# A new order for the first four sequences of a transformer block with routed experts, and scaled heads written by GpSimd in the first

## The chip, the cores and the metric

The kernel runs on one core of a Trainium2 chip. Its five engines each work off their own queue in order: TensorE (PE for matmuls, PEld for the loading of weights into the array), VectorE (DVE), ScalarE (ACT), GpSimd (POOL) and SyncE (SP, which here only issues DMAs). They wait for one another by semaphores. The metric is the device time of one execution in microseconds, the median of several runs.

## The reference

There are 16 sequences of 256 tokens with 256 features. Each goes through attention with 16 heads of 64, q and k normalised head by head; then all 4096 tokens are routed to 8 experts, 512 tokens each.

```python
shift = silu(t) @ W_ada.T + b_ada
h = ln(x, ln1_g, ln1_b) + shift
qkv = (h @ Wqkv.T).reshape(b, n, 3, H, HD)
q = ln(qkv[:, :, 0], qn_g, qn_b); k = ln(qkv[:, :, 1], kn_g, kn_b); v = qkv[:, :, 2]
attn = softmax(q @ k.T / sqrt(HD))
x = x + (attn @ v) @ Wout.T
gate = softmax(x @ Wgate.T)
vals, idx = top_k(gate.T, tokens // E)
g = ln(x[idx], mlp_g, mlp_b)
y = gelu(g @ fc1s.T + b1s) @ fc2s.T + b2s
out = x.at[idx].add(y * vals)
```

## The kernel before

Everything is in fp32. The weights of q, k and v lie in SBUF as one tile, `wq`, of six groups of 512 columns: groups 0 and 1 are q, 2 and 3 are k, 4 and 5 are v. A sequence has two token tiles, t = 0 and 1. I write a group of a token tile as (g, t).

At the start the groups of q and k are centred in place: `center(g, c)` (L548) takes the mean of each head's 64 columns from the columns, one half of the 256 input features (c = 0 or 1) at a time, by a VectorE sum (L552) and a VectorE subtraction (L553). So the projected heads have mean zero, and the norm of a head needs only the sum of its squares.

The steps of a sequence are methods of small classes:

- `First` (L578): statistics of a token tile of x (L563 to L567), the power -1/2 on GpSimd (L82), the normalising on VectorE (L573), transposes (L597), and ScalarE's eviction to `hT` with gain and shift (L605).
- `Group` (L619), for (g, t): `matmul` (L631) projects into the PSUM tile `pm`; a matmul for each half of the features. For v, ScalarE copies `pm` out (L640). For q and k: `square` on ScalarE (L644), `stats` on VectorE (L648, L652), `power` on GpSimd (L82), `scale` (L664), `transposes` on TensorE (L673) and `evict` on ScalarE with gain and bias (L685).
- `Quad` (L693), for four heads: `scores` (L706), the row maxima on VectorE (L713), the exponentials with their sums on ScalarE (L722), the reciprocals (L729), the normalising on GpSimd (L733), transposes (L742), copies (L750 on VectorE, L752 on ScalarE), and the product with v (L760).
- `Tail` (L775): the output projection (L784), the residual, the store, the second norm and the gate.

A group of q or k has two forms of `scale`. Without `keep`, VectorE reads `pm` and writes the scaled heads to `qk`. With `keep`, ScalarE has first copied `pm` to `qk`, and GpSimd multiplies `qk` in place:

```python
def keep(self):
    self.qk = work.tile([P, GW], F32, tag="qk", bufs=3, name="qk")
    nc.scalar.copy(self.qk, self.pm)
```

`pm`, the transposed heads and the transposed tokens share one PSUM tag, "mm", of three buffers; the scores and the transposed probabilities share "sc", of four. There are three buffers of `qk`.

The order of the work is written out by hand, as places. Every step has a number; `at` (L1177) pairs the places of a class with its steps, and the list of all, sorted by number, is carried out in that order, each step adding its instructions to its engines' queues. A place says where in the queues a step stands; it isn't a time that anything waits for. `zip` in `at` pairs no step with a place that isn't there: a group with seven places has no `keep`, one with eight has.

`STEADY` (L146) holds the places of one sequence, shifted by `PERIOD` for each later one. `START` (L191) replaces them for the first sequences: wholly for 0 and 1, the norm and the groups for 2, the norm for 3. `END` does the same for the last ones. `SHIFT`, `CENTER`, `FILL` and `LOADS` (L302 to L305) place the shift, the centring, some transposes of the identity that only keep TensorE occupied, and the loads that ScalarE's queue issues (x of later sequences, half of `wq`, `wo`). Sequence 15 has groups of eight places, all others seven.

Of the kernel before, what the change touches and what calls it, by code (L numbers as in the profile page):

```python
# [43 lines left out]
def kernel(  # L44
# [81 lines left out]
    def make_others():  # L126
# [20 lines left out]
        first=((-88.131, -77.795, -66.865), (-86.413, -85.278, -65.341), (-64.291, -63.624)),  # L147
# [42 lines left out]
    )  # L190
    START = {  # L191
        0: dict(
            first=((-139.487, -139.084, -130.002), (-134.729, -123.135, -95.026), (-71.635, -61.204)),
            group={
                (0, 0): (-59.500, -57.180, -53.990, -41.905, -41.892, -31.199, -19.864),
                (0, 1): (-56.514, -46.937, -42.187, -36.541, -32.975, -14.723, -12.430),
                (1, 0): (-11.345, -10.160, -10.123, -9.363, -7.717, 16.862, 17.870),
                (1, 1): (-17.061, -12.458, -10.932, -9.433, -9.429, -7.544, -7.063),
                (2, 0): (-47.944, -39.268, -37.967, -29.426, -29.083, -19.329, -15.473),
                (2, 1): (-36.593, -35.280, -31.121, -27.896, -26.496, -20.716, -17.116),  # L200
                (3, 0): (-0.195, 1.354, 5.032, 6.866, 7.484, 18.359, 20.756),
                (3, 1): (-7.052, -4.047, -4.021, -2.780, 5.168, 9.583, 16.657),
                (4, 0): (-61.161, -56.511),
                (4, 1): (-24.033, -19.174),
                (5, 0): (8.030, 14.550),
                (5, 1): (-0.065, 4.397),
            },
            quad={
                (0, 0): (-9.254, 22.590, 42.649),
                (0, 0, 0): (-4.098, 3.192, 35.521, 40.175, 42.160),  # L210
                (0, 0, 1): (-7.788, -2.839, 22.830, 27.700, 30.119),
                (0, 1): (-10.825, 1.530, 42.650),
                (0, 1, 0): (-9.045, -8.059, 15.256, 16.378, 17.222),
                (0, 1, 1): (-6.921, -0.152, 15.562, 17.096, 23.635),
                (1, 0): (0.126, 14.031, 62.413),
                (1, 0, 0): (5.581, 9.438, 28.540, 45.916, 48.521),
                (1, 0, 1): (6.615, 11.701, 34.709, 42.123, 45.511),
                (1, 1): (6.647, 32.947, 62.414),
                (1, 1, 0): (12.684, 22.346, 38.667, 41.778, 42.977),
                (1, 1, 1): (16.709, 24.888, 35.995, 40.496, 41.536),  # L220
                (2, 0): (36.613, 44.084, 79.640),
                (2, 0, 0): (38.678, 40.096, 53.301, 75.810, 75.857),
                (2, 0, 1): (37.844, 41.179, 46.653, 73.800, 78.092),
                (2, 1): (31.788, 44.810, 79.641),
                (2, 1, 0): (35.309, 35.316, 47.104, 63.762, 75.398),
                (2, 1, 1): (35.999, 36.383, 45.887, 51.730, 53.463),
                (3, 0): (57.532, 66.273, 80.859),
                (3, 0, 0): (62.041, 62.092, 75.830, 76.948, 78.262),
                (3, 0, 1): (58.897, 62.045, 71.274, 78.272, 80.335),
                (3, 1): (42.288, 56.582, 80.861),  # L230
                (3, 1, 0): (53.169, 56.538, 74.699, 79.614, 79.641),
                (3, 1, 1): (55.287, 56.039, 56.589, 75.724, 78.348),
            },
            out=(52.169, 77.187, 79.720, 81.968),
            tail=((83.431, 83.938, 98.840, 128.374, 103.780, 103.911, 108.593, 110.466), (101.110, 104.350, 128.872, 145.215, 106.950, 107.929, 158.941, 161.116)),
        ),
        1: dict(
            first=((-46.775, -2.928, 1.521), (-17.063, -5.314, 0.982), (15.343, 17.672)),
            group={
                (0, 0): (18.719, 22.736, 28.212, 28.786, 33.289, 38.005, 45.577),  # L240
                (0, 1): (21.654, 25.091, 29.577, 30.657, 37.616, 45.616, 50.362),
                (1, 0): (56.965, 58.830, 59.835, 62.211, 62.315, 70.246, 74.608),
                (1, 1): (56.747, 57.357, 58.840, 58.862, 61.374, 62.457, 62.468),
                (2, 0): (40.127, 40.864, 42.252, 42.262, 45.473, 48.208, 52.717),
                (2, 1): (40.977, 41.918, 42.391, 45.462, 46.160, 49.170, 52.410),
                (3, 0): (74.826, 75.081, 75.503, 78.958, 80.988, 81.454, 84.690),
                (3, 1): (72.447, 74.612, 74.727, 79.840, 80.430, 81.825, 83.328),
                (4, 0): (36.938, 40.518),
                (4, 1): (52.802, 53.597),
                (5, 0): (63.613, 73.243),  # L250
                (5, 1): (30.152, 33.881),
            },
            quad={
                (0, 0): (80.434, 81.692, 98.968),
                (0, 0, 0): (80.662, 81.021, 85.076, 94.133, 94.171),
                (0, 0, 1): (80.458, 80.463, 87.029, 93.291, 94.064),
                (0, 1): (58.862, 78.602, 98.969),
                (0, 1, 0): (66.341, 68.024, 80.857, 85.468, 86.358),
                (0, 1, 1): (68.231, 73.899, 80.721, 81.679, 85.268),
                (1, 0): (80.676, 90.848, 105.478),  # L260
                (1, 0, 0): (81.477, 86.038, 92.163, 96.097, 96.147),
                (1, 0, 1): (82.096, 83.656, 93.097, 94.720, 94.811),
                (1, 1): (88.704, 93.176, 105.479),
                (1, 1, 0): (88.738, 92.999, 95.490, 103.218, 105.069),
                (1, 1, 1): (89.119, 89.714, 93.216, 99.811, 103.812),
                (2, 0): (87.127, 91.001, 112.620),
                (2, 0, 0): (87.343, 88.876, 92.124, 103.385, 105.927),
                (2, 0, 1): (87.397, 89.577, 94.021, 106.117, 107.673),
                (2, 1): (97.984, 99.909, 112.621),
                (2, 1, 0): (97.999, 98.450, 100.142, 107.055, 108.977),  # L270
                (2, 1, 1): (99.110, 99.138, 100.960, 105.621, 106.739),
                (3, 0): (104.738, 110.015, 121.526),
                (3, 0, 0): (105.837, 106.636, 110.756, 113.604, 116.432),
                (3, 0, 1): (106.309, 108.745, 110.059, 117.644, 117.997),
                (3, 1): (98.364, 104.978, 121.527),
                (3, 1, 0): (100.330, 101.404, 107.082, 108.878, 110.458),
                (3, 1, 1): (101.810, 102.324, 111.030, 115.380, 116.157),
            },
            out=(99.694, 108.037, 114.478, 121.947),
        ),  # L280
        2: dict(
            first=((14.779, 25.231, 54.912), (8.366, 37.062, 43.204), (56.764, 58.743)),
            group={
                (0, 0): (76.135, 78.537, 79.284, 80.073, 81.775, 92.853, 94.460),
                (0, 1): (86.065, 86.151, 86.371, 86.494, 90.513, 100.607, 102.738),
                (1, 0): (97.900, 98.023, 98.876, 99.334, 101.083, 108.588, 109.754),
                (1, 1): (99.552, 100.917, 100.935, 100.939, 103.765, 109.148, 114.215),
                (2, 0): (80.956, 82.580, 82.606, 83.027, 83.166, 86.029, 88.107),
                (2, 1): (92.816, 93.215, 94.312, 94.328, 98.305, 102.746, 104.145),
                (3, 0): (118.246, 120.897, 121.729, 121.739, 125.070, 134.647, 136.279),  # L290
                (3, 1): (104.183, 104.593, 105.142, 106.832, 107.066, 112.897, 117.208),
                (4, 0): (89.871, 89.886),
                (4, 1): (91.705, 92.213),
                (5, 0): (90.505, 91.515),
                (5, 1): (106.951, 108.771),
            },
        ),
        3: dict(
            first=((47.228, 83.201, 107.818), (73.608, 96.452, 102.635), (108.887, 108.932)),
        ),  # L300
    }
    SHIFT = (-103.533, (-96.272, -72.697), (-98.034, -88.980))  # L302
    CENTER = ((-64.072, -68.386), (-36.649, -27.859), (-57.938, -59.128), (-18.701, -14.089))
    FILL = (16, 4, 8, 12)
    LOADS = (-61.203, -19.863)  # L305


    END = {
        12: dict(
            tail=((747.192, 755.581, 778.455, 793.120, 768.716, 771.682, 797.160, 797.956), (784.519, 787.608, 791.406, 797.787, 789.463, 793.641, 821.185, 824.781)),  # L310
        ),
        13: dict(
            quad={
                (0, 0): (718.441, 730.722, 765.251),
                (0, 0, 0): (726.260, 726.660, 736.012, 745.374, 749.979),
# [160 lines left out]
    if True:  # L476
# [764 lines left out]
        first = Routing()  # L1241
# [151 lines left out]
```

## Time and profile before

| what | value |
|---|---|
| three runs | 1186.35, 1189.59, 1192.12 us; median 1189.59 |
| the profiled execution | 1187.28 us, its span 1185.6 us |
| granted TensorE clock, mean | 0.994 |
| instructions in the span | 19672 |
| POOL L82, power of 8 heads | 128 x 1656 ns |
| ACT L644, square, 128x512 | 128 x 600 ns |
| ACT L722, Exp, 128x256 | 512 x 474 ns |
| DVE L648, sum of squares | 128 x 683 ns |

The page of a profile gives the busy time of each engine, the span in 40 slices, the DMA queues, and the costliest groups of instructions with their mean time and the idle time before them. The trace behind it answers more: the same groups in a stretch of time, who waited for whom, and the instructions in order of time. PE's ends are modelled, since matmuls are pipelined; the distance from one start to the next is the firmer number. Times are from the start of the span.

In the first 60 us the profile has these:

| stretch, us | PE busy | DVE busy | ACT busy | POOL busy |
|---|---|---|---|---|
| 0 to 20 | 16.67 | 13.14 | 4.95 | 6.34 |
| 20 to 40 | 17.97 | 17.39 | 13.29 | 10.29 |
| 40 to 60 | 20.00 | 11.79 | 16.13 | 13.18 |

### The profile page before, as it was taken

To read this page: it belongs to the slowest core of one execution; us is meant where nothing else is said; L and a number is where in the kernel's file an instruction comes from. 1 tells how busy PE (TensorE), PEld (TensorE's weight loads), DVE (VectorE), ACT (ScalarE), POOL (GpSimd) and SP (SyncE) were. 2 spreads that over 40 slices of the span, in tenths; PEclk is the share of its full clock that TensorE was granted. 3 is DMA by queue.
4 is the path that set the end of the run, shared out by engine and by line. 5 is a ranking of instruction groups with operands and counts; after the bars stand their busy time and mean duration, and the time that the engine had idled before them with its cause. 6 is when DMAs were issued, how large, how long until landed. Compare 5 with 4: busy or idle time off the path is not lost. (4 is left out here: it accounts for less than half of the span.)

```text
span 1185.6 us, 19672 instructions
## 1 busy us (share of the span) xinstructions
PE 1157.4 (98%) x6823; PEld 817.5 (69%) x6823; DVE 759.0 (64%) x2303; ACT 630.4 (53%) x1721; POOL 585.4 (49%) x813
## 2 busy tenths in 40 slices
PE   8999999999999999999999999999988899999996
PEld 5566666666666666666666666677745788888885
DVE  7665676667566666666666666565588578755540
ACT  3856655566565656565655565656566333233331
POOL 3665464556556455555555545463672143333332
PEclk9999999999999999999999999999999999999998
DMA  6000000000000000000000000000110365666661
GB/s 197 1 1 6 5 19 19 10 19 10 19 23 6 23 10 19 10 23 6 23 10 27 10 10 9 19 14 19 61 39 1 113 190 183 187 187 187 183 187 21
DMA packets 46740, 62.41 MB, mean 53 GB/s; under 512 B 3889, under 2 KB 39985, under 8 KB 46641
## 3 DMA queue, kind: packets, MB, share of 16 engines
q1 hardware_dynamic: 36864, 49.03, 12.4%
q0 software_dynamic: 6144, 8.39, 3.9%
q10 hardware_dynamic: 3632, 3.74, 1.0%
q8 instruction: 54, 0.88, 0.3%
q14 instruction: 46, 0.37, 0.1%
HBM read 48.56 MB, written 12.58 MB: 52 GB/s over the span
## 5 line engine op out<-in xcount | busy, mean ns | idle before, releaser
L631 PE MATMUL pm<-wq,hT 128*128 128x512 f32 x768 | 361.8, 600 | 2.2 <-ACT qT L685 0.9
L733 POOL TENSOR_SCALAR pr<-pr,sums 128x256 f32<-128x256 f32 x512 | 236.9, 480 | 208.3 <-DVE sums L729 160.9
L82 POOL TENSOR_TENSOR ss<-ss,neghalf 128x8 f32<-128x8 f32 x128 | 211.8, 1656 | 184.7 <-DVE ss L652 180.0
L722 ACT ACTIVATE pr<-sc,nmax 128x256 f32<-128x256 f32 x512 | 236.2, 474 | 115.9 <-DVE nmax L713 108.3
L631 PEld LDWEIGHTS pm<-wq,hT 128*128 128x128 f32 x768 | 133.6, 190 | 123.4 <-issue 109.9
L713 DVE TENSOR_REDUCE nmax<-sc 128x2 f32<-128x512 f32 x256 | 166.7, 684 | 38.2 <-PE sc L706 38.1
L648 DVE TENSOR_REDUCE ss<-sq 128x8 f32<-128x512 f32 x128 | 87.4, 683 | 109.9 <-ACT sq L644 109.4
L742 PEld LDWEIGHTS pp<-ident,pr 128*128 128x128 f32 x1024 | 119.1, 142 | 48.2 <-POOL pr L733 21.0
L742 PE MATMUL pp<-ident,pr 128*128 128x128 f32 x1024 | 139.2, 274 | 0.1
L644 ACT ACTIVATE sq<-pm 128x512 f32<-128x512 f32 x128 | 76.7, 600 | 113.5 <-PE pm L631 110.1
L706 PE MATMUL sc<-kT,qT 64*128 64x256 f32 x1024 | 129.3, 390 | 0.0
L760 PE MATMUL po<-prT,v 128*64 128x256 f32 x1024 | 126.1, 389 | 0.0
L706 PEld LDWEIGHTS sc<-kT,qT 64*128 64x128 f32 x1024 | 93.3, 186 | 41.9 <-issue 31.1
L784 PE MATMUL pw<-wo,oT 128*128 128x256 f32 x512 | 117.8, 383 | 0.0
L1135 PE MATMUL ph<-xT,w 128*128 128x256 f32 x512 | 117.5, 382 | 0.0
L1151 PE MATMUL py<-w,hid 128*128 128x256 f32 x512 | 116.5, 380 | 0.0
L1168 POOL DMA_INDIRECT out<-y,idx x32 | 51.4, 1605 | 124.8 <-DVE y L1162 57.7
L784 PEld LDWEIGHTS pw<-wo,oT 128*128 128x128 f32 x512 | 96.7, 192 | 18.7 <-issue 6.5
L722 ACT ACTIVATION_READ_ACCUMULATOR pr<-sc,nmax 128x1 f32 x512 | 105.0, 205 | 0.0
L1142 ACT ACTIVATE hid<-ph,vec 128x256 f32<-128x256 f32 x128 | 60.2, 473 | 83.3 <-PE ph L1135 75.8
L1135 PEld LDWEIGHTS ph<-xT,w 128*128 128x128 f32 x512 | 95.4, 190 | 12.9
L1151 PEld LDWEIGHTS py<-w,hid 128*128 128x128 f32 x512 | 95.5, 190 | 12.7
(136 smaller groups left out, 1294.1 us busy)
## 6 DMA issues: line engine op xcount, KB each, us to landing
w<-in_fc2T SPq DMA_DIRECT2D x16, 1024.0 KB
w<-in_fc1T SPq DMA_DIRECT2D x16, 1024.0 KB
out<-tok SPq DMA_DIRECT2D x32, 128.0 KB
xn_dram<-tn SPq DMA_DIRECT2D x32, 128.0 KB
xs<-in_x SPq DMA_DIRECT2D x12, 256.0 KB
b<-in_b2s SPq DMA_DIRECT2D x16, 128.0 KB
wq<-in_wqkvT SPq DMA_DIRECT2D x3, 512.0 KB
wq<-in_wqkvT ACTq DMA_DIRECT2D x3, 512.0 KB
```

What stands on the lines that cost most here:

```text
L82: nc.gpsimd.tensor_tensor(dst, src, neghalf[:, : src.shape[1]], ALU.pow)
L631: nc.tensor.matmul(self.pm, hTs[self.b][:, c, bass.ts(self.t, P)], wq[:, c, bass.ts(self.g, GW)], start=(c == 0), stop=(c == DC - 1),)
L648: nc.vector.tensor_reduce(self.ss[:, 0, :], self.sq.rearrange("p (h d) -> p h d", d=HD), AX.X, ALU.add,)
L706: nc.tensor.matmul(self.sc[i, j][:, t, :], qTs[self.b][rows, hp, bass.ts(t, P)], kTs[self.b][rows, hp, :], start=True, stop=True,)
L713: nc.vector.tensor_reduce(self.nmax[i, j], self.sc[i, j], AX.X, ALU.max, negate=True)
L722: nc.scalar.activation(self.pr[i, j][:, t, :], self.sc[i, j][:, t, :], AF.Exp, bias=self.nmax[i, j][:, t : t + 1], scale=1.0, accum_out=se ...
L733: nc.gpsimd.tensor_scalar(self.pr[i, j][:, t, :], self.pr[i, j][:, t, :], self.sums[i][:, 1, j, t : t + 1], 1.0, ALU.mult, ALU.mult,)
L742: nc.tensor.transpose(self.pp[i, j][:, c, bass.ts(t, P)], self.pr[i, j][:, t, bass.ts(c, P)], ident,)
L760: nc.tensor.matmul(self.po[j * HD : (j + 1) * HD, i, :], vs[self.b][:, c, bass.ts(4 * self.d + 2 * i + j, HD)], self.prT[i, j][:, c, :], s ...
L784: nc.tensor.matmul(self.pw, oTs[self.b][:, hp, bass.ts(self.t, P)], wo[:, hp, :], start=(hp == 0), stop=(hp == HP - 1),)
L1135: nc.tensor.matmul(self.ph[f], self.w1[:, c, bass.ts(f, P)], self.xT[:, c, :], start=(c == 0), stop=(c == DC - 1),)
L1151: nc.tensor.matmul(self.py[i], self.hid[:, f, bass.ts(i, P)], self.w2[:, f, :], start=(f == 0), stop=(f == FC - 1),)
```

## The change

Only places change. The eight groups of q and k of sequence 0 get an eighth place, so `keep` runs for them and GpSimd scales them; and all places of the sequences 0 to 3 that `START` holds are new, as are those of the shift, the centring and the two sets of loads. The number of sequences, all sizes, buffers and steps are as before, and so are `STEADY` and `END`. The core of it:

```diff
         0: dict(
-            first=((-139.487, -139.084, -130.002), (-134.729, -123.135, -95.026), (-71.635, -61.204)),
+            first=((-133.593, -101.058, -97.256), (-158.376, -131.500, -104.051), (-81.952, -81.887)),
             group={
-                (0, 0): (-59.500, -57.180, -53.990, -41.905, -41.892, -31.199, -19.864),
-                (0, 1): (-56.514, -46.937, -42.187, -36.541, -32.975, -14.723, -12.430),
-                (1, 0): (-11.345, -10.160, -10.123, -9.363, -7.717, 16.862, 17.870),
-                (1, 1): (-17.061, -12.458, -10.932, -9.433, -9.429, -7.544, -7.063),
-                (2, 0): (-47.944, -39.268, -37.967, -29.426, -29.083, -19.329, -15.473),
-                (2, 1): (-36.593, -35.280, -31.121, -27.896, -26.496, -20.716, -17.116),
-                (3, 0): (-0.195, 1.354, 5.032, 6.866, 7.484, 18.359, 20.756),
-                (3, 1): (-7.052, -4.047, -4.021, -2.780, 5.168, 9.583, 16.657),
-                (4, 0): (-61.161, -56.511),
-                (4, 1): (-24.033, -19.174),
-                (5, 0): (8.030, 14.550),
-                (5, 1): (-0.065, 4.397),
+                (0, 0): (-80.466, -69.038, -57.316, -39.709, -38.352, -36.469, -35.382, -52.242),
+                (0, 1): (-60.059, -54.606, -54.600, -39.627, -32.905, -30.429, -30.229, -51.780),
+                (1, 0): (-30.395, -29.479, -6.942, 7.553, 11.559, 18.176, 30.532, -20.763),
+                (1, 1): (-33.879, -30.714, -22.761, -17.147, 0.473, 1.479, 6.362, -30.403),
+                (2, 0): (-51.648, -51.234, -47.356, -33.810, -32.220, -27.888, -16.240, -49.845),
+                (2, 1): (-39.169, -35.673, -32.084, -31.658, -31.069, -18.625, -11.081, -36.449),
+                (3, 0): (-15.423, -2.636, 4.458, 12.729, 16.826, 29.832, 31.195, 2.002),
+                (3, 1): (-20.569, -12.443, -7.775, 1.095, 1.104, 10.131, 14.846, -2.034),
+                (4, 0): (-81.874, -62.410),
+                (4, 1): (-47.993, -40.422),
+                (5, 0): (2.941, 10.417),
+                (5, 1): (-35.340, -32.229),
             },
             quad={
-                (0, 0): (-9.254, 22.590, 42.649),
+                (0, 0): (-10.378, 16.013, 65.445),
...
-                (0, 1): (-10.825, 1.530, 42.650),
+                (0, 1): (-1.606, 22.773, 65.446),
...
-    SHIFT = (-103.533, (-96.272, -72.697), (-98.034, -88.980))
-    CENTER = ((-64.072, -68.386), (-36.649, -27.859), (-57.938, -59.128), (-18.701, -14.089))
+    SHIFT = (-103.258, (-99.231, -92.324), (-94.650, -91.422))
+    CENTER = ((-91.311, -88.593), (-42.094, -51.590), (-84.871, -62.797), (-31.921, -44.332))
     FILL = (16, 4, 8, 12)
-    LOADS = (-61.203, -19.863)
+    LOADS = (-81.886, -35.381)
```

In the queues this means, for the first projections on TensorE:

```
before: (4,0) fill (0,0) (0,1) (2,0) (2,1) T(0,0) (4,1) T(2,1) T(2,0) (1,1) T(0,1) (1,0) scores ...
after:  (4,0) fill (0,0) (0,1) (2,0) (4,1) (2,1) T(0,0) (5,1) (1,1) T(0,1) (1,0) T(2,0) (3,1) T(2,1) (3,0) scores ...
```

T(g,t) stands for the transposes of the scaled heads.

## The prediction

> **What bounds the kernel now.** I read the engines' busy times first, then cut the span into stretches, then asked what TensorE waited for in the first 45 us.
>
> ```profile
> PE 1157.4 (98%) x6823; PEld 817.5 (69%) x6823; DVE 759.0 (64%) x2303; ACT 630.4 (53%) x1721; POOL 585.4 (49%) x813
> ```
>
> ```profile
> 0.00:12.00 12.00, 9.52 (x57) 8.04 (x58) 5.70 (x16) 2.53 (x4) 1.86 (x9) 1.00 0.82 262
> 12.00:32.00 20.00, 17.12 (x65) 8.55 (x65) 17.64 (x37) 8.84 (x14) 9.44 (x6) 1.00 0.42 135
> 32.00:45.00 13.00, 13.00 (x61) 7.61 (x60) 10.65 (x26) 11.73 (x37) 7.94 (x12) 1.00 0.00 1
> 45.00:850.00 805.00, 805.00 (x4655) 534.19 (x4654) 516.45 (x1170) 483.28 (x1381) 445.24 (x661) 1.00 0.04 14
> ```
>
> The columns are the stretch, its length, busy time of PE, PEld, DVE, ACT and POOL, granted clock, DMA. From 32 to 850 us TensorE is never idle, so there a new order can only lose. The stretch after 850 (336 us, 312.78 busy) is the end, which stays and moves along. What can be won lies before 32 us: 2.88 idle in 12:32 and 2.48 in 0:12.
>
> TensorE's waits in 0:45, as line, releaser, total, times, longest:
>
> ```profile
> PE pq L673 <- DVE qk L664: 1.3, 2, 1.0
> PE pm L631 <- ACT qT L685: 0.9, 1, 0.9
> PE pm L631 <- DVE wq L553: 0.7, 1, 0.7
> PE pm L631 <- DVE qk L664: 0.7, 1, 0.7
> ```
>
> A group's PSUM tile is read twice: ACT squares it, then, after DVE's sum and POOL's power, DVE scales it. The three "mm" tiles are held through that chain, so TensorE stands. One rule says otherwise of what bounds the kernel: the Trainium skill, Perfetto Trace Analysis, section Identifying the Most-Contended Engine, says that matmul busy time misjudges TensorE and weight-load busy time judges its room. By the rule 69% leaves 31% of room, some 360 us, and a better order could win much anywhere. But the weight loads of one projection start at 12.29, 12.71, 13.14, 13.57: one pass per 0.43 us, each with a load of 0.19 and 0.24 of "issue". That stream is full at 44% load. I take the row: no room after 32 us.
>
> **Costs used**, all from the timeline: a projection is four passes, 1.72 us, readable 2.02 after its start (11.75 to 13.77). Four transposes occupy 0.43 (42.05, 42.49, 42.93), readable after 0.66 (20.79 to 21.45). Eight score matmuls take 1.93 (37.10 to 39.03). ACT starts 512-wide work every 0.50 (13.77, 14.27), a head's eviction every 0.68. Centring half a weight group is two DVE instructions, 1.33. A power is 1.64. The new pair exists already, in the last sequence:
>
> ```profile
> L664 DVE TENSOR_TENSOR qk<-pm,ss x120: 658/681/693, 17.1 to 817.7; 128x512 f32<-128x512 f32 x120
> L664 POOL TENSOR_TENSOR qk<-qk,ss x8: 1042/1042/1228, 835.3 to 877.4; 128x512 f32<-128x512 f32 x8
> L626 ACT COPY qk<-pm x8: 580/584/620, 833.6 to 872.5; 128x512 f32<-128x512 f32 x8
> ```
>
> So DVE loses 8 x 0.68 = 5.4 us, ACT gains 8 x 0.58 = 4.7, POOL gains 8 x 1.04 = 8.3. POOL's sequence-0 line goes from 8 x 1.64 = 13.1 to 21.4. A PSUM tile is now free after two ACT instructions.
>
> **The new beginning, step by step.** Up to 9.16 nothing moves: same loads, shift, first transposes, first projection (4,0), and the 12 fills end at 11.06.
>
> *Centring.* Before, half 1 of group 0 was centred before half 0, and the projection begins with half 0, so it waited to 11.75. Now half 0 comes first (done 10.37), half 1 at 11.70, needed 0.86 after the start. (0,0) starts at 11.08: 0.67 won.
>
> *Projections.* (0,0) 11.08, (0,1) 12.80, (2,0) 14.52 (its weights centred at 14.35), (4,1) 16.24 (ACT has copied (0,0) away at 15.90), (2,1) 17.96 to 19.68. None waits.
>
> *First heads.* POOL: power of (0,0) 15.24 to 16.88, of (0,1) to 18.60, scale of (0,0) to 19.62. Its transposes run 19.69 to 20.12. Before they ran at 20.79 with one projection fewer done: TensorE is 1.1 + 1.72 = 2.8 us ahead.
>
> *The added waits.* There are three "qk" tiles, so ACT's copy of (2,1) waits for the transposes of (0,0) (20.35), with the square of (2,1), the eviction of (0,0) and the loads behind it; the square then gives DVE its sum at 21.45, while DVE is centring anyway.
>
> *A new stop.* (5,1) runs 20.15 to 21.87. Then (1,1) needs group 1 centred. DVE, from 16.96: half 1 of group 1, a sum, statistics of sequence 1, half 1 of group 3, half 0 of group 1: done 22.75. TensorE waits 0.9.
>
> *The port.* Here a rule speaks against the change. The Trainium skill, SBUF — State Buffer, section Who interferes with whom: a DVE instruction with two SBUF inputs and a GpSimd instruction that reads SBUF exclude each other for a whole instruction. Centring's second half (L553) has two. Against POOL's powers the trace shows nothing (L553 is 0.691 to 0.693 in all eight). Against POOL's scale there is one near row, a DVE product of two SBUF tiles:
>
> ```profile
> 854.69 2.23 POOL L664 TENSOR_TENSOR qk<-qk,ss 128x512 f32<-128x512 f32 x2
> 854.78 1.36 DVE L852 TENSOR_TENSOR gate_of<-gates,smax 128x224 f32<-128x224 f32 x1
> ```
>
> It ends 0.4 after the first of the two scales: it seems to have stood until then, and the scales lost 0.15 (2.23 against 2.08). So row and rule agree in kind; the size depends on who meets whom. The last centring (22.06) falls into the scale of (0,1), 21.26 to 22.28: by the row 0.22 late; without the rule 0; if it stood through the next scale too, 1.25. I take 0.2: TensorE resumes at 23.0.
>
> *To the scores.* (1,1), transposes of (0,1) (scaled 22.3), (1,0), transposes of (2,0) (23.3), (3,1), transposes of (2,1) (26.3), (3,0): all scaled 2.1 us or more before TensorE arrives, ACT's releases too. Four projections and three transposes are 8.2: scores start at 31.2. Before they started at 29.0 with 8 projections done; now 11 are, and as many transposes: 3 x 1.72 - 2.2 = 3.0 ahead. Before then loses 0.4 more at 31.4 (waiting for the scaled (1,1)): 3.4.
>
> *After the scores.* POOL's scales of (1,1), (3,1), (1,0) end near 31, 33.5, 36.2, each 2.3 to 3.5 before use. ACT becomes the late one. Its queue, in order: square and copy of (3,0) and (3,1), the Exp table load (1.28, at 29.74 before), two Exps, the copy of (3,0), two Exps, the eviction of (1,1), V, sequence 1's hT. On the copy of (3,0) hang sequence 1's first transposes; on the eviction, those of (3,1); on hT, the first projection of sequence 1. From the square of (3,0) at 31.5 I get: copy of (3,0) done 35.35, the second Exps 36.25, hT's first half 38.0, against TensorE's 35.28, 36.05, 37.5. Stops: 0.1, 0.2, 0.5. By 45 us: 3.4 - 0.8 = 2.6 ahead.
>
> *45 to 50.* The second eight scores need PSUM tiles that two more Exp pairs and a copy release at 46.9 and 47.4: 0.5. POOL waits for the first statistics of sequence 1 with three normalisations queued behind; their transposes come 3 us later. Sum: **2.1 us**.
>
> *Moved loads.* The x, wo loads on ACT's queue still follow the first head's eviction (21.45 before, 21.4 now). DVE asks for sequence 2's statistics earlier, at 24.8; x0 took 3.1 us from its issue at 0.79 to use, so x2 is there at 24.5. If not, the sums of (1,1) wait; they have 2 us. SP keeps its order but for two stores exchanged.
>
> DVE's 5.4 and ACT's 4.7 count nothing by themselves: neither sets the end. Of sequences 1 to 3 the order is new too; I found no number there, TensorE has 100% before, so the bounds are 0 and a loss. I take 0, as POOL (445 of 805 us) and ACT (483) have room in that stretch.
>
> **Sum.** The profiled execution took 1187.28 (span 1185.6); less 2.1 is 1185.2. The runs' median is 1189.59, 2.3 above it, within their spread of 1186.35 to 1192.12. So the forecast is 1187.5. About 0.5%, 5.9 us, is what a measurement can tell from no change, and this is 0.2%. The most that could come is 0.67 plus what TensorE loses between 11.75 and 45. By 43.47 it has done 12 projections, 8 head transposes, 16 scores and three more fours: 29.3; less the first two pieces (2.15) that is 27.15 in 31.72: 4.57. So 5.2 us, below 0.5%.
>
> **Rivals.**
> *Given back (0.27).* The order up to sequence 4 has stops that the old one hadn't: ACT's queue slips by a few more places like the one at hT. For it: ACT has 11.73 of 13 us in 32:45 and gets 3 of the copies there or just before. Against: later it has 40% free. A loss equal to the win gives 1189.6.
> *POOL becomes the line (0.12, the slower one).* Every scale blocks or is blocked by DVE's two-input work, and power plus scale are strictly in order. At 2 x 1.04 each, eight cost 8.3 more; 2.1 are slack; 6.2 stops against 2.6 won: 3.6 slower, 1193.2. It decides from 0.6 per scale on (8 x 0.6 = 2.1 + 2.6). With 0.69 before and after each, 11 - 2.1 - 2.6 = 6.3: 1195.9. For it: the 1.36 row. Against: only four centrings remain then, and the scales in the last sequence are 1.04 in the median.
> *The stops of this sum are larger (0.06).* The port 1.25 instead of 0.2, hT and the second scores 1.5 each instead of 0.5: 3.05 more, 1190.5.
> The forecast has 0.55.
>
> **Numbers.** The likeliest case alone runs from 1184.4 (all 5.2) to 1188.8. For 8 in 10 I take 1184.0 to 1192.5, which takes in given back, most of the POOL case and the runs' own spread. Faster by over 0.5% would need more than there is: 0.03, for a shifted median. Slower by over 0.5%: 0.09, the bad end of the POOL case and a stop in sequences 1 to 3 that I don't see.
>
> **What would show it.** TensorE's first long projection run starts near 11.1; first head transposes near 19.7; a wait on L553 of about 1 near 22; scores near 31.2; 12:32 busy near 18.9; no wait on L664 by POOL longer than 0.3. POOL's scales at 1.04 to 1.2 refute the slower rival; scales near 2 and TensorE waiting for them make me wrong, and so does idle TensorE between 45 and 220.

## The result, and the profile after

The changed kernel's median is 1184.52 us (5 runs, 1184.28 to 1187.2), that of before beside it 1190.09 (5 runs, 1186.35 to 1192.12); the ratio is 0.9959, with a 95% interval of 0.9943 to 0.9975. In a second comparison, with 9 runs against 31, it is 0.9972 (0.9960 to 0.9985). The change makes the kernel about 0.3 to 0.4% faster, 3.4 to 5.6 us in the medians. Forecast were 2.1 us. The profiled execution, though, took 1187.2 us with a span of 1185.5: it shows nothing of the gain against the 1187.28 and 1185.6 of before. That is the riddle of this case.

First the busy line of the page of the changed kernel, then its stretches (length, busy PE, PEld, DVE, ACT, POOL, granted clock, DMA):

```profile
PE 1160.5 (98%) x6823; PEld 820.6 (69%) x6823; DVE 755.6 (64%) x2295; ACT 634.3 (54%) x1729; POOL 595.7 (50%) x821
```

```profile
0.00:12.00 12.00, 10.54 (x44) 9.27 (x45) 6.22 (x17) 2.53 (x4) 1.87 (x9) 1.00 0.70 228
12.00:32.00 20.00, 19.38 (x67) 9.86 (x66) 14.90 (x34) 10.69 (x20) 14.17 (x12) 1.00 0.47 156
32.00:45.00 13.00, 13.00 (x64) 7.49 (x64) 7.65 (x19) 12.08 (x36) 11.66 (x13) 1.00 0.00 1
45.00:850.00 805.00, 805.00 (x4668) 535.12 (x4665) 518.08 (x1171) 484.80 (x1385) 447.22 (x661) 1.00 0.04 14
```

In 12:32 TensorE is now idle for 0.62 us instead of 2.88, and from 32 to 850 it never is, as before. Of its waits before 850 us, beside that for the first fill, one is left:

```profile
PE pm L631 <- ACT qT L685: 0.6, 1, 0.6
```

So the waits went as meant. What ate the gain stands ahead of 12 us. The timeline of TensorE in this execution:

```profile
5.14 1.86 PE L512 MATMUL pa<-sT,wa 128*128 128x16 f32 x8
6.84 1.09 PE L499 MATMUL fill<-ident 128*128 128x128 f32 x4
7.72 1.06 PE L597 MATMUL ph<-ident,xn 128*128 128x128 f32 x4
8.58 1.91 PE L499 MATMUL fill<-ident 128*128 128x128 f32 x8
```

Eight fills take 1.91 us here; in the profile of before they took 1.04, from 6.94 on. TensorE ran at half its speed until after 10 us here, and only up to about 5 us there. I call an execution warm early or warm late by this. The first long run of projections thus starts at 13.64, not at 11.1. The same kernel, profiled a second time:

```profile
5.14 1.03 PE L512 MATMUL pa<-sT,wa 128*128 128x16 f32 x8
6.03 0.63 PE L499 MATMUL fill<-ident 128*128 128x128 f32 x4
6.62 0.66 PE L597 MATMUL ph<-ident,xn 128*128 128x128 f32 x4
7.11 1.04 PE L499 MATMUL fill<-ident 128*128 128x128 f32 x8
...
11.06 2.31 PE L631 MATMUL pm<-wq,hT 128*128 128x512 f32 x5
```

To compare executions apart from this I use an anchor: the transposes of one later sequence's normed tokens (L597), which stand in the steady order of every kernel here; ahead of them each trace has the same 2202 matmul records, fills aside. The timeline near 400 us of before, of the changed kernel, and of its second profile:

```profile
406.30 0.60 PE L597 MATMUL ph<-ident,xn 128*128 128x128 f32 x4
```

```profile
406.06 0.60 PE L597 MATMUL ph<-ident,xn 128*128 128x128 f32 x4
```

```profile
403.92 0.60 PE L597 MATMUL ph<-ident,xn 128*128 128x128 f32 x4
```

With TensorE fast early in both, the changed kernel is 406.30 - 403.92 = 2.4 us ahead (3.0 ahead of before's second profile, whose first weights came later, see below). With TensorE fast late it is still 0.2 ahead of an execution of before that was fast early.

### The profile page after: what moved, and what is told of

Same layout as the page of the kernel before. It is cut to its first block, busy times and chain, and to the rows that moved or that the text cites. A ratio compares the mean times of both kernels' runs of the same rounds, so it can differ in the third digit from the quotient of the medians.

```text
span 1185.5 us, 19697 instructions
## 1 busy us (share of the span) xinstructions
PE 1160.5 (98%) x6823; PEld 820.6 (69%) x6823; DVE 755.6 (64%) x2295; ACT 634.3 (54%) x1729; POOL 595.7 (50%) x821
## 3 DMA queue, kind: packets, MB, share of 16 engines
q1 hardware_dynamic: 36864, 49.03, 12.5%
```

## The experiments

The table has each kernel's profiled execution (start of the first long run of projections, anchor, anchor less start) and all its runs. Before ran 84 times beside them: 1186.28 to 1192.35, mean 1189.5. Two theories on the variation between executions are named in what was expected: W puts it down to the moment near the start at which TensorE becomes fast, D to falls of the clock that short waits of TensorE bring. What they call equal warm-up is the comparison of executions that are both warm early or both warm late.

| kernel | start | anchor | difference | median of runs | ratio to before (95%) |
|---|---|---|---|---|---|
| before, first profile | 11.75 | 406.30 | 394.55 | 1190.09 | |
| before again | 12.37 | 406.91 | 394.54 | 1189.84 | 1.000 (0.9988 to 1.0012) |
| changed, first profile | 13.64 | 406.06 | 392.42 | 1184.52 | 0.9959 (0.9943 to 0.9975) |
| changed again | 11.06 | 403.92 | 392.86 | 1186.67 | 0.9972 (0.9960 to 0.9985) |
| centring only | 11.04 | 407.23 | 396.19 | 1189.76 | 0.9999 (0.9985 to 1.0012) |
| order without copies | 13.03 | 426.88 | 413.85 | 1206.13 | 1.0129 (1.0111 to 1.0146) |
| copies without order | 11.90 | 412.91 | 401.01 | 1194.01 | 1.0043 (1.0027 to 1.0059) |
| scales doubled | 10.96 | 408.71 | 397.75 | 1190.01 | 1.0004 (0.9994 to 1.0014) |
| group 1 centred early | 13.20 | 404.77 | 391.57 | 1184.98 | 0.9958 (0.9942 to 0.9973) |
| fewer fills | 10.34 | 403.16 | 392.82 | 1185.32 | 0.9972 (0.9960 to 0.9984) |
| before, gaps filled | 12.15 | 406.70 | 394.55 | 1187.40 | 0.9982 (0.9969 to 0.9995) |
| both mends | 11.04 | 403.62 | 392.58 | 1184.56 | 0.9964 (0.9950 to 0.9978) |
| three mends | 12.59 | 404.13 | 391.54 | 1184.56 | 0.9957 (0.9942 to 0.9973) |
| no first fills | 14.11 | 406.53 | 392.42 | 1187.41 | 0.9984 (0.9971 to 0.9997) |

### Before again, and changed again

No edit.

> The kernel before, unchanged. The changed kernel was 5.6 us faster in the medians, but its profiled execution took 1187.2 and starts its projections at 13.64 us, 2.6 later than I worked out: TensorE still ran each filling transpose in 0.22 us up to about 10 us, where the profile of before had 0.12 from 5 us on. Theory W (warm-up): the moment at which TensorE gets fast differs from execution to execution of one kernel and shifts all after it; then the times of this kernel spread over 4 us or more, with low ones near 1187 and high ones near 1190 to 1192, and an execution with late fast transposes is long. Theory O (order): the order alone is worth 5 us at equal warm-up and 1187.2 was a stray; then this kernel's times lie within 2 us of 1190. Both expect a ratio of 1.000.

> The changed kernel, unchanged. Theory W: where TensorE is fast from 5 us on, the first long run of projections starts at 11.1 and the span is near 1182.8; where it is fast only from 10 us on, 13.6 and 1185.5; at equal warm-up it is 2.1 to 2.9 us ahead of before. Theory O: 4 to 5.6 us ahead of before whatever the warm-up. Ratio 0.9945 to 0.998 in both.

Before's 14 runs spread over 5.3 us, from 1186.64 to 1191.96: that is a spread as theory W expects, but W is not shown to be its cause. The profiled execution, 1189.6, is 2.3 us longer than the first profile of before, and TensorE was warm early in both. What differs at the start is a wait for centring, which was 0.69 in the first:

```profile
12.37 5.42 PE L631 MATMUL pm<-wq,hT 128*128 128x512 f32 x12 [1.30 <-DVE wq L553]
```

VectorE's first centring sum, which waits for the load of `wq`, began at 9.58 instead of 8.96: 0.6 us come from there, and 1.7 from behind the anchor. None of the five profiles with before's beginning (the two here, centring only, copies without order, gaps filled) is warm late, so what late warmth costs before was not seen. The changed kernel's second profile has TensorE fast at 5 us and its long run at 11.06, as theory W has it, and is 2.4 ahead at the anchor, within 2.1 to 2.9. Its span missed: 1185.1 instead of 1182.8. What follows the anchor took 1185.1 - 403.92 = 781.2 there and 779.3 to 779.4 in the first profiles of both kernels; the order there is the same. So a further 2 us of variation lie in the end. Theory O, 4 us or more whatever the warm-up, is refuted by the anchor.

### Centring only

```diff
-    CENTER = ((-64.072, -68.386), (-36.649, -27.859), ...
+    CENTER = ((-68.386, -64.072), (-36.649, -27.859), ...
```

> The kernel before with one thing changed: of group 0, half 0 is centred before half 1. Theory W and the working of the prediction: 0.67 us where TensorE is fast early, nothing where it is fast late, since the fills then end after both halves are centred; ratio 0.9994 to 1.000, and the profile has no wait of TensorE on L553. If the centring is what set the beginning, 2 us or more.

The wait on L553 is gone and the first long run starts at 11.04, 0.7 earlier; the time is the same. The profile shows a second thing: the gaps that remain cost the clock. TensorE's timeline and the stretches of this kernel:

```profile
17.30 1.98 PE L631 MATMUL pm<-wq,hT 128*128 128x512 f32 x4 [0.94 <-DVE qk L664]
20.11 0.63 PE L673 MATMUL pq<-ident,qk 128*128 128x128 f32 x4 [0.82 <-DVE qk L664]
21.60 2.94 PE L631 MATMUL pm<-wq,hT 128*128 128x512 f32 x4 [0.87 <-ACT qT L685]
```

```profile
18.00:21.00 3.00, 1.92 (x7) 0.64 (x6) 2.93 (x7) 0.82 (x2) 1.83 (x3) 1.00 0.00 0
21.00:24.00 3.00, 2.40 (x4) 1.05 (x5) 2.93 (x6) 0.55 (x1) 1.56 (x1) 0.75 0.66 180
24.00:27.00 3.00, 3.00 (x12) 2.19 (x11) 2.64 (x6) 2.11 (x3) 0.00 (x0) 0.68 1.05 363
```

After three waits within 6 us the granted clock fell to 0.75 and 0.68 in two stretches of 3 us, and the projection at 21.60 took 2.94 instead of 1.98. The difference of the anchor is 1.6 us more than in the two profiles of before, which had waits of the same kind (0.66, 0.97 and 0.87 in both) and no fall of the clock. So such gaps sometimes cost a clock dip and sometimes don't.

### Order without copies

```diff
-                (0, 0): (-80.466, -69.038, -57.316, -39.709, -38.352, -36.469, -35.382, -52.242),
+                (0, 0): (-80.466, -69.038, -57.316, -39.709, -38.352, -36.469, -35.382),
...
```

> The changed kernel without its eight copies: VectorE scales the heads of sequence 0 out of PSUM, all other places as changed. If early release of PSUM by the copies carries the gain: TensorE waits on L664 for the fourth and fifth projection and after, 2 us or more are lost against the changed kernel, and it is not faster than before (1188 to 1194). If the order alone carries it: within 1 us of the changed kernel.

It lost 16 us against before, far more than expected. TensorE's waits:

```profile
PE pm L631 <- DVE qk L664: 6.0, 1, 6.0
PE pq L673 <- DVE qk L664: 4.0, 3, 3.3
```

A projection stood 6.0 us for a PSUM tile that the late scale held, and the granted clock was 0.50 in 24:30 and 45:48. The new order isn't usable without the early release.

### Copies without order

```diff
-                (0, 0): (-59.500, -57.180, -53.990, -41.905, -41.892, -31.199, -19.864),
+                (0, 0): (-59.500, -57.180, -53.990, -41.905, -41.892, -31.199, -19.864, -57.179),
...
```

> The kernel before with its own places, and the eight copies added right behind the squares, so that GpSimd scales the heads of sequence 0. If copies and order are needed together (my theory): POOL works the heads in the old order, power and scale in turn, 15.4 + 4 x 2.7 = 26.1 for the fourth, whose transposes stand second in the old order, after the fifth projection; TensorE reaches them near 20.8 and stands about 5 us; 3 to 5 us are lost against before, 1192 to 1195, and the granted clock dips in 12:32. If the early release of PSUM alone carries the gain: within 1 us of the changed kernel.

```profile
PE pq L673 <- POOL qk L664: 6.5, 2, 6.2
```

TensorE stood 6.2 us at the second transposes, expected were about 5, and the granted clock fell as expected (0.50 in 27:30). The runs are in the range expected. Copies and order each lose alone and win together.

### Scales doubled

```diff
+                if self.b == 0:
+                    extra = work.tile([P, GW], BF16, tag="extra", bufs=1, name="extra")
+                    nc.gpsimd.tensor_tensor(extra, src, self.ss[:, 1, :], ALU.mult)
                 engine.tensor_tensor(
```

(with the views of the scale itself)

> The changed kernel with a second GpSimd product per head of sequence 0, into a tile that nobody reads, so that a scale costs about 2.1 instead of 1.04 us. By the prediction's slack of 2.1 us (four heads at the scores, 2.3 to 3.5 for the later ones): TensorE waits 5 to 7 us more for GpSimd by 45 us, and the kernel is 4 to 7 us slower than the changed one, slower than before by 1 to 4. If GpSimd has much more room than that: less than 2 us slower than the changed kernel.

```profile
PE pq L680 <- POOL qk L671: 4.2, 5, 1.5
```

TensorE now waits in five places for GpSimd, 4.2 us in sum, and the anchor's difference is 4.9 to 5.3 above the changed kernel's. The runs are 3.5 above its 14 runs' median of 1186.5 (4.3 in the means), and level with before: a little less than expected. So the rival's mechanism is right and its slack nearly so, and its premise, a scale of 2 us, is what didn't come.

### Group 1 centred early, fewer fills, and both

```diff
-    CENTER = ((-91.311, -88.593), (-42.094, -51.590), ...
-    FILL = (16, 4, 8, 12)
+    CENTER = ((-91.311, -88.593), (-51.595, -51.590), ...
+    FILL = (16, 4, 8, 4)
```

> The changed kernel with half 0 of group 1 centred ahead of half 1, right behind the second sum, instead of last of four. Where the wait near 22 is that centring's: TensorE goes through (5,1) to (1,1) without the 1.06 us, the third head's sum and power come 1.3 later, the transposes of (0,1) still find their scale (22.3 + 1.3 against 23.9); 0.8 to 1.0 faster than the changed kernel at equal warm-up. If the wait is ACT's, as the profile's row names it: no gain.

TensorE has no wait left but that for the first fill. The row of the changed kernel that names ACT's eviction as the releaser was, then, about VectorE's centring. At equal (late) warm-up 0.85 are gained, 392.42 to 391.57.

> The changed kernel with 4 instead of 12 filling transposes behind the first projection. Where TensorE is fast early, the first long run starts at 11.1 as before, since the centring sets it; where it is fast late, at 12.7 instead of 13.6: 0 to 1 us faster in the median. If the fills there hold the clock up: the granted clock dips below 1 in 9:18 and the kernel is 1 us or more slower.

The clock held. The first long run started at 10.34 in this execution, which was warm early, so the 12 fills, and not the centring, had set 11.06; the expectation had that the other way round. In the runs there is no difference that the intervals tell from the changed kernel.

> The changed kernel with group 1's half 0 centred early and 4 instead of 12 fills: each took 0.8 to 1 us off the changed kernel at equal warm-up. If they add: 1.7 to 2 us less than the changed kernel at equal warm-up, median 1183.5 to 1184.8, faster than both kernels. If they meet (an earlier first run finds group 1 not yet centred): 0.8 to 1.2.

Warm early, as here, the mends meet: TensorE now waits for centring (0.5 in two places) where it didn't before, and the anchor moves by 0.3 only.

### Three mends

```diff
-                (5, 0): (2.941, 10.417),
+                (5, 0): (2.941, 12.303),
```

> As both mends, and ScalarE copies V of (5,0) after sequence 1's hT instead of before it. If the stop of 0.5 us at sequence 1's first projection is ScalarE's queue: another 0.4 to 0.5, median 1183.0 to 1184.4. If the copy held back keeps a PSUM tile: no gain or a loss up to 0.5.

No wait is left in its profile, but the 0.4 to 0.5 didn't come. The anchor's difference is 391.54, against 391.57 with group 1 centred early, which was warm late too and has the copy of V in its old place. ScalarE's hT now begins 5.45 us after the scores, where it began 5.91 after them in the changed kernel's second profile; sequence 1's first projection begins 6.55 after them and began 6.57:

```profile
31.60 2.00 PE L706 MATMUL sc<-kT,qT 64*128 64x256 f32 x16
37.05 1.05 ACT L605 ACTIVATE hT<-ph,bias,vec 128x256 f32<-128x256 f32 x2
38.15 1.98 PE L631 MATMUL pm<-wq,hT 128*128 128x512 f32 x4
```

So hT was not what that projection waited for, or not alone; what was, stays open. The ratio is the lowest of all, level with group 1 centred early; its interval lies below before and overlaps that of the changed kernel, whose 14 runs have a mean of 1186.1 against 1184.5. It is not shown to be better than the change.

### Before, gaps filled

```diff
             at([p + 0.001], partial(fill, n))
+        for n, p in ((4, -36.594), (8, -31.200), (8, -24.034)):
+            at([p], partial(fill, n))
```

> The kernel before with 4, 8 and 8 filling transposes (their results unused) in the three places of 17 to 22 us where TensorE stands, so that it is busy there and does no more work. Theory D (dips): of the 3.6 us by which the executions differ in the mean, 2.4 are waits that the new order takes away at equal warm-up, and the rest is the granted clock falling to a half in 21:27 in some executions of before, as in the profile with only the centring exchanged (0.75 and 0.68 there, 1.6 us lost). Then this kernel's mean falls by 1 to 1.5 us against before's 1189.6, to 1188.1 to 1188.6, and no execution is above about 1191, with no dip in its profile. If dips are rare in before: the mean stays within 0.4 of 1189.6, or rises by the fills' surplus of 0.1 to 0.3.

Stretch 12:32 of this kernel:

```profile
12.00:32.00 20.00, 19.15 (x82) 10.71 (x83) 17.64 (x37) 8.72 (x13) 9.05 (x6) 1.00 0.43 140
```

TensorE is idle for 0.85 us in place of 2.88 and does no more useful work: the anchor's difference is 394.55, to 0.01 that of before. Yet the mean of 12 runs is 1187.3 against 1189.25 of the 31 runs of before beside them, 1.9 less, and the highest is 1188.93 against 1192.35. Where the clock fell in those runs is not recorded, but each run's mean granted clock is:

| runs | clock 0.994 or 0.995: runs, mean us | clock 0.993 or below: runs, mean us |
|---|---|---|
| before, all 84 | 29, 1187.3 | 55, 1190.6 |
| before, the 31 beside this kernel | 15, 1187.4 | 16, 1191.0 |
| before, gaps filled | 12, 1187.3 | none |
| changed, both comparisons | 9, 1185.4 | 5, 1187.2 |

Two thirds of before's executions have a lower clock, and they take 3.3 us longer in the mean. With the gaps filled no execution has, and the mean is that of before's executions with the higher clock. A mean clock counts falls anywhere in a run, but the edit adds fills in the gaps and nothing else. So the gaps bring falls of the clock, as theory D says, and most of before's spread goes with them: at the higher clock all 29 runs lie within 2.3 us. The size, 1.9, was more than the 1 to 1.5 expected.

### No first fills

```diff
-    FILL = (16, 4, 8, 12)
+    FILL = (0, 4, 8, 12)
```

> The changed kernel without the 16 filling transposes at the very start; the work of the start comes at the same time, since it waits for loads. If TensorE's speed depends on how long it has been busy: it is slow in nearly every execution up to 9 us or more, the profile's first long run starts at 12.5 to 13.7, and nearly all executions lie in the upper part of the changed kernel's range: median 1187 to 1188.5, 0.5 to 2 us slower than the changed kernel. If the speed comes by chance alone: no difference.

The first long run starts at 14.11, and all 12 runs lie between 1186.75 and 1189.05, where the changed kernel's 14 lie between 1184.28 and 1188.43. TensorE ran at half its speed until 12 us, longer than in any other profile, and the start is later than the 12.5 to 13.7 expected. One profile and 12 runs speak for it that how long TensorE has been busy counts. With the fills the moment still differs between executions of one kernel; nothing here shows by what.

## Why the prediction was right

The forecast 1187.5 is 3 us above what was measured, within the range given; faster and "within 0.5%" came as the likeliest case had it. The gain was larger than the 2.1 forecast: 5.6 us in the medians of the first comparison, 3.4 in the means of all runs. The 5.6 is in part luck: all five runs of the changed kernel there had a mean clock of 0.994 or 0.995, while five of the nine in the second comparison had less. The steps, against the second profile, the one with early warm-up:

```profile
19.65 0.60 PE L673 MATMUL pq<-ident,qk 128*128 128x128 f32 x4
20.08 1.88 PE L631 MATMUL pm<-wq,hT 128*128 128x512 f32 x4
23.03 1.96 PE L631 MATMUL pm<-wq,hT 128*128 128x512 f32 x4 [1.06 <-ACT qT L685]
...
31.38 2.00 PE L706 MATMUL sc<-kT,qT 64*128 64x256 f32 x16
...
37.29 1.07 ACT L605 ACTIVATE hT<-ph,bias,vec 128x256 f32<-128x256 f32 x2
37.95 1.98 PE L631 MATMUL pm<-wq,hT 128*128 128x512 f32 x4
```

- *Centring*: start 11.06, worked out 11.08. In 12:32 TensorE is busy for 18.94, worked out 18.9.
- *First heads*: 19.65 for 19.69, six projections done.
- *A new stop*: (1,1) at 23.03 for 23.0. It is VectorE's centring, as said, shown by the kernel with group 1 centred early.
- *The port*: 0.2 were taken, 0.13 came. The rows of the second profile:

```profile
18.36 1.04 POOL L664 TENSOR_TENSOR qk<-qk,ss 128x512 f32<-128x512 f32 x1
18.53 0.90 DVE L652 TENSOR_SCALAR ss<-ss 128x8 f32<-128x8 f32 x1
...
21.11 2.72 POOL L664 TENSOR_TENSOR qk<-qk,ss 128x512 f32<-128x512 f32 x2
22.11 0.82 DVE L553 SCALAR_TENSOR_TENSOR wq<-ws,wq 128x512 f32<-128x512 f32 x1
```

L553 took 0.82 instead of 0.69, and GpSimd's pair of scales 2.72 instead of 2.08. Neither reached TensorE beyond that. That a small L652 took 0.90 instead of 0.17 was not forecast; it has one SBUF tile as input, and ended with the scale beside it (19.43 and 19.40).
- *To the scores*: 31.38 for 31.2. *After the scores*: sequence 1's first projection at 37.95 for 38.0. ScalarE's own times were read rightly: the copy of (3,0) was done at 35.37 for 35.35, the second Exps at 36.20 for 36.25, hT's first half at 37.90 for 38.0. That TensorE stops for hT is not borne out: three mends has hT earlier, and the projection came no sooner. There the number was right for a reason that isn't shown.
- *Sequences 1 to 3*: no idle TensorE between 32 and 850, as taken.
- *The whole, warm early in both*: 2.4 for 2.1, from one execution each; 3.0 against before's second profile, of which 0.6 is its later load.

The step that was off is *Sum*: it carried the difference of two executions over to the medians by adding the 2.3 us that lay between before's profiled execution and its median. That 2.3 was put down to spread alone. In part it was the cost of the same gaps: in most executions the clock is lower, and filling the gaps with idle work takes these executions and 1.9 us of the mean away (ratio 0.9982). Of the profiles with gaps as short as before's, one shows the fall itself, that of centring only; that it lies there in the other runs too follows from the filling, not from a trace of them. The change takes most of the gaps away, and with them part of that. So the term "what TensorE loses between 11.75 and 45", 4.57 in one execution, is larger in the mean. Of the rivals, given back didn't happen, and GpSimd didn't become the line; doubled scales show that it would have.

The means differ by 3.4 us (1189.5 over 84 runs against 1186.1 over 14). At a mean clock of 0.994 or 0.995 they differ by 1.9 (1187.3 against 1185.4), near the 2.1 forecast; the other 1.5 are the lower clock, which 55 of before's 84 runs have and 5 of the changed kernel's 14. What stays open is how many executions of each kernel are warm late, which the runs without a profile don't tell, and with 14 runs the two parts are rough.

## What to carry to other kernels

Where one engine is busy all the rest of the time, a new beginning is worth the gaps that it closes there, and the steps can be worked out to 0.2 us from rows of the old trace. Copying a PSUM tile away early and reordering the work that needs the tile belong together: each alone lost 4 and 16 us here. Before a profile's time is set against a median, see from the length of equal matmuls whether that execution was warm at the same moment, and sort the runs by their mean granted clock. A gap in TensorE's work can cost more than its length.

## What the hardware showed

- TensorE's speed at the start is a matter of the execution. In the profiles that are warm late, four transposes took 1.06 to 1.09 us where they took 0.60 to 0.66 in those that are warm early, of the same kernel too. By the starts of the single matmuls, TensorE became fast at 4.3 to 5.9 us in nine profiles and at 9.7 to 10.9 in four, all with the same first fills from 1.44 on. The Trainium skill, TensorE: Matmul & The Clock Gate, section Part 1, says that a free-running activity window of some 3.4 us decides, with the phase left to chance. The trace agrees with the factor of two and with a moment that differs between executions; the window itself no run here shows. Late warmth cost the changed kernel 2.1 us at the anchor (406.06 against 403.92).
- In those first 10 us the granted clock stands at 1.00 in the profile's rows although the transposes took twice their time; the falls at 21:27 of centring only do show there.
- Three waits of 0.8 to 0.9 us within 6 us were followed by a clock of 0.75 and 0.68 in 21:27. Filling such gaps with unused transposes left no run with a mean clock below 0.994, of 12, where 16 of 31 had one.
- In the end of the kernel, with its order unchanged, the stretch after the anchor took 777.7 to 781.2 us over the profiles. The granted clock is below 1 between 900 and 950 us each time (0.83 to 0.94 in before, 0.66 and 0.83 when it was profiled again, by stretches of 10 us). Added up as 10 us times what is missing to 1, that is 3.4 to 3.5 us in eleven profiles with ends of 777.7 to 779.4, and 5.1 in the two second profiles, with ends of 781.0 and 781.2; order without copies, with 6.8 and 779.9, doesn't fit in. This is a further part of the spread.
